# Four joined edits to a four-layer graph kernel: shared PSUM banks in the recurrent gates, and three moved steps

## The chip, the cores and the metric

One Trainium2 chip, one of its cores. The metric is device time in microseconds for one execution of the whole program. A run is timed several times and the median is given. A profile of one execution comes beside it.

## What is computed

Input x is 128 graphs of 64 nodes with 256 features, with one adjacency matrix of 64x64 for all. Four layers follow, each `x = layernorm(x + layer(x))`:

```python
x = _layernorm(x + _L0_gnn_ref(x, adj, ...))   # dense attention: softmax over neighbours
x = _layernorm(x + _L1_gnn_ref(x, ...))        # 4-head attention over 512 edges, segment softmax
x = _layernorm(x + _L2_gnn_ref(x, adj, ...))   # A_hat x, W1, batchnorm, relu, W2, batchnorm
x = _layernorm(x + _L3_gnn_ref(x, adj, ...))   # two graph convolutions, then windowed LSTMs
```

The last layer is the long one. After its two graph convolutions it runs, for each length p from 1 to 4, an LSTM over windows of p nodes and writes the last hidden state back into h:

```python
def step(carry, x_t):
    h, c = carry
    g = x_t @ Wih.T + h @ Whh.T + bias
    i, f, gg, o = jnp.split(g, 4, axis=-1)
    c = jax.nn.sigmoid(f) * c + jax.nn.sigmoid(i) * jnp.tanh(gg)
    h = jax.nn.sigmoid(o) * jnp.tanh(c)
...
for p in range(1, MAX_SKIP + 1):
    nw = Tv // p
    wins = h[:, :nw * p, :].reshape(Bv * nw, p, Hd)
    last = _lstm_last(Wih[p - 1], Whh[p - 1], bih[p - 1], bhh[p - 1], wins)
    idx = jnp.arange(nw) * p + (p - 1)
    h = h.at[:, idx, :].set(last.reshape(Bv, nw, Hd))
```

All is float32.

## The kernel before

The order of instructions is mostly written out by hand. `given` (L121 is its line) makes what it traces on an engine come after what it traced last on that engine; `step` does the same for TensorE alone in layers 0 and 1, and `behind` for one engine and its latest instruction. Where neither is used, the compiler's planner orders an engine's instructions. Each engine then works through its own list in order and waits for the others by semaphores.

**Layers 0 and 1** are one loop over 16 tiles `q` of 512 rows, with eight slots per tile. A slot has one `l1_graph` product (bank "z", two buffers) and then the steps listed in `between`. They belong to other tiles: `l0_a` to `l0_e` attention of layer 0 one or two tiles ahead, `l1_t`, `l1_qv` the projections of the next tile, `l1_softmax`, `l1_sums`, `l1_weights` once for two tiles, and `v_a`, `v_b`, `v_c` the values, the output projection with its normalisation, and layer 2's neighbour sums, a few tiles behind. Small results go through bank "m", three buffers. `v_c` fills a "z" bank and ScalarE copies it out (L491). `v_a` fills two "m" banks and ScalarE copies them out as yT (L456).

**Layer 2** is made of two products with weights, done for pairs of tiles by a Strassen-Winograd scheme: seven products in place of eight, with sums of the inputs (`tile_sums`: one subtraction on VectorE, three on GpSimd) and of the weights (`weight_sums`). While the last tiles of layer 1 end, the loop over `v_a, v_b, v_c` is filled with such products from the list `fill`. The sums use rooms that an earlier pair's sums held.

**Layer 3** begins with four blocks `gcn` of the two graph convolutions (a generator: scaling, two normalisations, neighbour sums, two products), interleaved by a hand-written list of block numbers. `first_sums` makes the weight sums of length 1 (four GpSimd subtractions, L1430) and stores them (L1432).

Then `lstm(pair)` handles 32 graphs at a time, four pairs in all. Length 1 is the class `Wide`. For lengths 2 to 4, each time step after the first has four gates f, g, i, o, a `Gate` each. A gate is again seven products: product j is made by `part(j, 0)`, with the input, and `part(j, 1)`, with the hidden state, both into one of six PSUM banks "l" (L1761). `use` then takes it out:

- products 1 and 5: ScalarE copies them to SBUF (L1776), `kept[1]` and `kept[5]`;
- product 2: VectorE adds `kept[1]` (L1778), the first quarter `t[0][:, 0]`;
- product 6: VectorE adds `kept[1]` (L1780); product 7: VectorE adds that (L1782); then `kept[5]` is added twice, for the second and fourth quarter (L1784, L1785), on GpSimd, for gate o on VectorE;
- product 4: VectorE adds `kept[7]` (L1787); product 3: VectorE adds it to the second quarter (L1789).

`act` applies sigmoid or tanh with the bias, in place (L1794), two quarters at a time; it runs in the next gate's time. `finish` and `tanh` follow with the cell. TensorE's order of the products in gates g and i is 1, 5, 2, 6, 7, 4, 3, in gate o 1, 5, 2, 6, 7, 3, 4. After gate o the first half of six products of the next step's gate f (`nxt`) is begun at once, while VectorE makes the hidden state (L1661) and its sums (L1625, L1626). Steps of other blocks (`gcn`, `final`, `prepare`) are put between gates by the table `side`.

Of the kernel before, what the change touches and what calls it, by code (L numbers as in the profile page):

```python
# [11 lines left out]
AF = mybir.ActivationFunctionType  # L12
# [7 lines left out]
N = 64  # L20
# [6 lines left out]
NQ = 16  # L27
# [14 lines left out]
def kernel(ctx: ExitStack, tc: tile.TileContext, i, out):  # L42
# [72 lines left out]
    def given(do, *args, **more):  # L115
        traced = nc.cur_bb.bb.instructions
        first = len(traced)
        with ExitStack() as order:
            for e in latest.values():
                order.enter_context(tc.issue_after(e))  # L120
            r = do(*args, **more)  # L121
        for t in traced[first:]:
            if t.engine in (mybir.EngineType.PE, mybir.EngineType.DVE, mybir.EngineType.Activation,
                            mybir.EngineType.Pool):
                latest[t.engine] = t
        return r
# [8 lines left out]
    with ExitStack() as two:  # L135
# [322 lines left out]
        def v_b(q):  # L458
# [12 lines left out]
                layernorm(x2, y, PQ, nc.gpsimd)  # L471
            nc.sync.dma_start(x2_dram[q], x2.rearrange("p c d -> p (c d)"))

        def v_c(q, one=True):

            x2 = L1.pop(q)["x2"]
            if one:
                both = bank([2, E], name="z", bufs=2)
                p_ = [both[:, s, :].rearrange("p (k c n) -> p k c n", k=KD, c=PQ) for s in range(2)]
            else:  # L480
                p_ = [bank([KD, PQ, N]) for _ in range(2)]
            for c in range(PQ):
                for k in range(KD):
                    for h in range(2):
                        for s in range(2):
                            r, f = slice(s * N, (s + 1) * N), slice(h * 64, (h + 1) * 64)
                            nc.tensor.matmul(p_[s][f, k, c, :], x2[r, c, k * P + h * 64:k * P + (h + 1) * 64],
                                             aht[r, r], start=True, stop=True)
            dst = Aq(q).rearrange("p (b s n) -> p s b n", b=KD * PQ, s=2)
            if one:  # L490
                nc.scalar.activation(dst, both.rearrange("p s (b n) -> p s b n", n=N), AF.Copy)  # L491
            else:
                for s in range(2):
                    nc.scalar.activation(dst[:, s], p_[s].rearrange("p k c n -> p (k c) n"), AF.Copy)
# [239 lines left out]
        for q in range(NQ):  # L734
            S = q // BPS - 1 if q % BPS == 0 else -1
            between = [
                [(l0_e, q + 1 if q else -1), (l0_a, q + 2)],
                [(l0_e, -1 if q else 1), (sums, q if q else -1), (l1_softmax, S)],
                [(l1_sums, S), (l0_b, q + 2)],
                [(v_b, q - LAG - 1)],  # L740
                [(l1_t, q + 1), (l1_weights, S), (l0_c, q + 2)],
                [(sums, q), (l1_qv, q + 1, 0)] + [(lambda n: behind(l0_x, n), q + 2)],
                [(v_c, q - LAG - 1), (v_a, q - LAG)],
                [(l0_d, q + 2), (l1_qv, q + 1, 1)],
            ]
            for b in range(GQ):
                step(l1_graph, q, b)
                for do, n, *more in between[b]:
                    step(do, n, *more)
                for do in setup.get((q, b), ()):  # L750
                    step(lambda _: behind(lambda _: do(), 0, mybir.EngineType.DVE), 0)
# [202 lines left out]
                    pass  # L954
            late.clear()

        def tile_sums(b):

            t2, t3, t4 = rooms[next(rooms_at) % len(rooms)]
            t1 = b(0, 1)  # L960
            given(nc.gpsimd.tensor_tensor, t3, b(1, 1), t1, OP.subtract)
            given(nc.vector.tensor_sub, t1, t1, b(0, 0))
            given(nc.gpsimd.tensor_tensor, t2, b(1, 1), t1, OP.subtract)
            given(nc.gpsimd.tensor_tensor, t4, b(1, 0), t2, OP.subtract)
            return [t1, t2, t3, t4]

        def sums_in_order(b):

# [9 lines left out]
        def inputs(q):  # L978
            return lambda k, n: Aq(q + n)[:, k * QT:(k + 1) * QT]
# [25 lines left out]
        for n, (do, q) in enumerate([(do, q) for q in range(NQ - LAG, NQ) for do in (v_a, v_b, v_c)]):  # L1005
            given(do, q, *[False] * (do == v_c))
            fill[n]()
            if n in sums_at:
                T[sums_at[n]] = tile_sums(inputs(sums_at[n]))
        q = NQ - LAST - 1  # L1010
        values.close()
        ps_b = two.enter_context(tc.tile_pool(name="ps_b", bufs=3, space=PSUM, side="right", reuse_waits="tile"))
# [28 lines left out]

        assert q == NQ - LAST - 1
        ends = range(NQ - LAST, NQ, 2)
        T = {ends[0]: tile_sums(inputs(ends[0]))}
        given(up_block, q)

        def finish(g):
# [362 lines left out]
    def gate_of(n):  # L1410
        return "ifgo".index(n), AF.Tanh if n == "g" else AF.Sigmoid
# [11 lines left out]
    def first_sums():  # L1423

        S = rooms_of(0)[1]
        a = wih1.rearrange("p k (g m c) -> p k g m c", g=3, m=2)
        a11, a12, a21, a22 = (a[:, k, :, m] for k, m in ((0, 0), (1, 0), (0, 1), (1, 1)))
        for dst, x, y, op in ((2, a11, a21, OP.subtract), (0, a21, a22, OP.add), (1, S[:, 0], a11, OP.subtract),
                              (3, a12, S[:, 1], OP.subtract)):
            nc.gpsimd.tensor_tensor(S[:, dst], x, y, op)  # L1430
        d = dram.tile([P, 3 * QT], F32, name="sums1")
        nc.sync.dma_start(d, S.rearrange("p j g c -> p (j g c)"))  # L1432
        sums_kept.append(d)

    def lstm(pair):
# [170 lines left out]
        for p in range(2, SKIP + 1):  # L1606
# [129 lines left out]
            class Gate:  # L1736


                def __init__(self, n, r, s, tiles):
                    self.n, self.r, self.s, self.tiles = n, r, s, tiles  # L1740
                    self.t = tiles[n] = rows()
                    self.banks, self.kept = {}, {}
                    self.at, _ = gate_of(n)

                def part(self, j, src):

                    if not src:
                        if j in self.banks:
                            return
                        self.banks[j] = lbank([nw, GB])  # L1750
                    r, s = self.r, self.s
                    a, S = w.raw[src], w.S[src]
                    lhs = {1: a[:, 0, self.at, 0], 2: a[:, 1, self.at, 0], 4: a[:, 1, self.at, 1]}.get(j)
                    if lhs is None:
                        lhs = S[{3: 3, 5: 0, 6: 1, 7: 2}[j]][:, self.at]
                    if j <= 3:
                        m, n = ((0, 0), (1, 0), (1, 1))[j - 1]
                        rhs = hid[:, m, n] if src else inp(r, s, m)[:, n]
                    else:
                        rhs = (hsums if src else xsums[r, s])[:, (3, 0, 1, 2)[j - 4]]  # L1760
                    nc.tensor.matmul(self.banks[j], lhs, rhs, start=src == 0, stop=src == 1)  # L1761

                def keep(self, j):
                    self.kept[j] = late.tile([P, nw, GB], F32, name="kept", bufs=5)
# [6 lines left out]

                def use(self, j):

                    b, k, t = self.banks[j], self.kept, self.t
                    if j in (1, 5):
                        nc.scalar.activation(self.keep(j), b, AF.Copy)  # L1776
                    elif j == 2:
                        nc.vector.tensor_add(t[0][:, 0], b, k[1])  # L1778
                    elif j == 6:
                        nc.vector.tensor_add(t[0][:, 1], b, k[1])  # L1780
                    elif j == 7:
                        nc.vector.tensor_add(self.keep(7), b, t[0][:, 1])  # L1782
                        e = nc.vector if self.n == "o" else nc.gpsimd
                        e.tensor_tensor(t[0][:, 1], t[0][:, 1], k[5], OP.add)  # L1784
                        e.tensor_tensor(t[1][:, 1], k[7], k[5], OP.add)  # L1785
                    elif j == 4:
                        nc.vector.tensor_add(t[1][:, 0], b, k[7])  # L1787
                    else:
                        nc.vector.tensor_add(t[0][:, 1], b, t[0][:, 1])  # L1789
# [14 lines left out]
            for r in range(len(runs)):  # L1804
                if p > 2:
                    yield "gap", unit
                for s in range(p):
# [16 lines left out]
                    else:  # L1824
                        names = "fgio"
                        for at, n in enumerate(names):
# [3 lines left out]
                            G.product(5)  # L1830
                            if prev:
                                prev.act(1)
                                prev.act(0)
                                prev.after(1)
                                G.product(2)
                                prev.after(0)
                                prev.tanh(1)
                            G.product(6)
                            if n == "o":
                                G.act(0, 0)  # L1840
                            if prev:
                                prev.tanh(0)
                            G.product(7)
# [86 lines left out]
    first = [prepare(weights_of[0, p]) for p in (2, 3)]  # L1930
    for p in (2, 3):
        weights_of[0, p].room()
    given(first_sums)
    for n in [0, 0, 0, 1, 1, 0, 1, 0, 0, 1, 2, 0, 0, 2, 1, 2, 1, 0, 3, 1, 1, 1]:
        given(next, parts[n])
    lstms = [lstm(k) for k in range(NP)]
    next(lstms[0])
    for n in [2, 3, 2, 3, 2]:
# [99 lines left out]
```

## Time and profile before

| | |
|---|---|
| median of 3 runs | 2018.45 us (2016.33 to 2020.31) |
| profiled execution | 2017.13 us |
| its span | 2015.4 us, granted TensorE clock 0.988 |
| TensorE matmul busy | 1932.2 us, 96% |
| VectorE | 1279.8 us, 64% |
| ScalarE | 952.3 us, 47% |
| GpSimd | 878.7 us, 44% |

The span goes from the first to the last instruction; the profiled execution's own time has 1.7 us more around it. Layers 0 and 1 end at about 490 us, layer 2 at about 735, and the lengths 2 to 4 of the first pair begin at about 840. In lines of the profile, "L1761 PE" is line 1761 on TensorE, PEld is TensorE's weight load, DVE is VectorE, ACT ScalarE, POOL GpSimd, SP SyncE. A tile is named out<-in, and the part in brackets is the engine's idle time before the instruction with what ended it.

### The profile page before, as it was taken

What the parts mean: (1) busy time and instruction counts of PE and PEld (TensorE: products, weight loads), DVE (VectorE), ACT (ScalarE), POOL (GpSimd) and SP (SyncE); (2) the same over time, 40 slices, a digit from 0 to 9 for tenths busy, and PEclk for the clock granted to TensorE, in tenths of its full rate; (3) what the DMA queues carried; (4) which work ended last, traced back from release to release, by engine and by line L of the source; (5) the groups of instructions that cost most, each with busy time, mean ns of one, the idle gap of its engine ahead of it and who ended that gap; (6) DMA issues with size and microseconds to landing.
All of it is one profiled execution on the core that took longest, in us unless ns stands there. A gap on an engine that the chain in (4) does not pass through costs nothing.

```text
span 2015.4 us, 31385 instructions
## 1 busy us (share of the span) xinstructions
PE 1932.2 (96%) x11447; PEld 1334.4 (66%) x11447; DVE 1279.8 (64%) x2858; ACT 952.3 (47%) x1663; POOL 878.7 (44%) x1016
## 2 busy tenths in 40 slices
PE   6899999998999989899999999999999999999996
PEld 5667777775544446577678577668577668578685
DVE  6767767664555655765657765566865557764566
ACT  4566665664336524544334644343644333544333
POOL 1133344334353633565445444345543435444264
PEclk9999999999999989999999999999999999999998
DMA  5354343322220134532333333132233032132022
GB/s 157 57 73 75 75 77 59 53 54 46 45 52 20 63 126 134 180 125 91 142 120 92 122 101 131 43 139 86 87 123 121 22 116 70 36 121 79 0 66 71
DMA packets 236538, 173.83 MB, mean 86 GB/s; under 512 B 150624, under 2 KB 213600, under 8 KB 233056
## 3 DMA queue, kind: packets, MB, share of 16 engines
q1 hardware_dynamic: 234528, 169.86, 29.9%
q8 instruction: 90, 1.47, 0.3%
q0 software_dynamic: 1024, 1.05, 0.2%
q10 hardware_dynamic: 832, 0.92, 0.1%
q14 instruction: 64, 0.52, 0.1%
HBM read 110.18 MB, written 61.60 MB: 85 GB/s over the span
## 4 chain that ended last, share of the span: by engine, by line
PE 75%; DVE 15%; ACT 3%; issue 2%; POOL 2%; DMA 2%; SPq 0%; DVEq 0%; POOLq 0%; ACTq 0%
PE l L1761 27%; PE l L1717 8%; PE pz L878 4%; PE l L1496 4%; PE m L343 3%; PE pz L807 3%; PE e L372 3%; PE z L381 2%; PE m L466 2%; PE m L346 2%; PE m L262 2%; PE g L1395 2%; PE g L1383 2%; PE pz L1076 2%; PE m L316 1%
## 5 line engine op out<-in xcount | busy, mean ns | idle before, releaser
L1761 PE MATMUL l<-hs,wh 128*128 128x256 f32 (+1 forms) x896 | 276.0, 399 | 3.7 <-DVE hs L1625 3.1
L1761 PE MATMUL l<-xs,wx 128*128 128x256 f32 (+1 forms) x896 | 276.1, 399 | 2.6 <-DVE gate L1780 2.6
L86 POOL TENSOR_TENSOR ln_rs<-ln_rs,mhalf 128x2 f32<-128x2 f32 (+2 forms) x98 | 86.3, 881 | 371.6 <-DVE ln_rs L98 365.6
L1776 ACT ACTIVATE kept<-l 128x256 f32<-128x256 f32 (+1 forms) x224 | 88.6, 402 | 333.5 <-PE l L1761 332.1
L1761 PE MATMUL l<-H,wx 128*128 128x256 f32 (+1 forms) x672 | 210.5, 402 | 4.5 <-DVE gate L1789 3.6
L1761 PE MATMUL l<-hid,wh 128*128 128x256 f32 (+1 forms) x672 | 208.8, 399 | 0.0
L1761 PEld LDWEIGHTS l<-hs,wh 128*128 128x128 f32 x896 | 169.1, 190 | 47.1 <-DVE hs L1625 5.7
L1761 PEld LDWEIGHTS l<-xs,wx 128*128 128x128 f32 x896 | 168.9, 190 | 45.7 <-POOL st L105 2.5
L1717 PE MATMUL l<-H,wx 128*128 128x256 f32 (+5 forms) x672 | 185.0, 431 | 4.9 <-DVE H L121 2.7
L1794 ACT ACTIVATE gate<-gate,bias 128x512 f32<-128x512 f32 (+1 forms) x280 | 170.6, 657 | 40.4 <-DVE gate L1785 34.5
L383 ACT ACTIVATE u<-z 128x1024 f32<-128x1024 f32 x128 | 130.2, 1024 | 75.6 <-PE z L381 74.9
L1717 PEld LDWEIGHTS l<-H,wx 128*128 128x128 f32 x672 | 118.8, 190 | 65.3 <-issue 34.4
L1761 PEld LDWEIGHTS l<-H,wx 128*128 128x128 f32 x672 | 125.7, 190 | 42.8 <-DVE gate L1789 7.6
L1761 PEld LDWEIGHTS l<-hid,wh 128*128 128x128 f32 x672 | 127.2, 190 | 32.0 <-issue 2.9
L1784 POOL TENSOR_TENSOR gate<-gate,kept 128x256 f32<-128x256 f32 (+1 forms) x84 | 65.0, 774 | 145.3 <-DVE kept L1782 144.9
L1789 DVE TENSOR_TENSOR gate<-l,gate 128x256 f32<-128x256 f32 (+1 forms) x112 | 49.9, 446 | 87.9 <-POOL gate L1784 62.1
L354 DVE TENSOR_TENSOR qs<-m,qs 64x256 fp32r<-64x256 f32 x128 | 54.0, 422 | 75.2 <-ACT qs L353 73.0
L381 PE MATMUL z<-gath_r,qs 128*128 128x512 f32 x256 | 100.6, 480 | 0.4 <-ACT u L383 0.3
L1629 POOL TENSOR_TENSOR hs<-hid 128x256 f32<-128x256 f32 (+1 forms) x28 | 26.0, 929 | 170.3 <-DVE hid L1661 87.2
L1683 ACT ACTIVATE gate<-cell 128x512 f32<-128x512 f32 (+1 forms) x88 | 58.6, 666 | 83.3 <-DVE cell L1675 60.4
L1671 POOL TENSOR_TENSOR cell<-gate,cell 128x512 f32<-128x512 f32 (+1 forms) x56 | 75.3, 1366 | 28.1 <-ACT gate L1794 28.1
L1778 DVE TENSOR_TENSOR gate<-l,kept 128x256 f32<-128x256 f32 (+1 forms) x112 | 49.1, 438 | 60.1 <-ACT gate L1794 32.7
(388 smaller groups left out, 4074.2 us busy)
## 6 DMA issues: line engine op xcount, KB each, us to landing
wx<-sums SPq DMA_DIRECT2D x9, 2048.0 KB
wh<-sums SPq DMA_DIRECT2D x9, 1792.0 KB
way<-st SPq DMA_DIRECT2D x54, 256.0 KB
st<-way SPq DMA_DIRECT2D x216, 64.0 KB
xin<-in_x SPq DMA_DIRECT2D x16, 512.0 KB
ld<-table SPq DMA_DIRECT2D x16, 512.0 KB
x_dram<-y SPq DMA_DIRECT2D x16, 512.0 KB
x2r<-x_dram SPq DMA_DIRECT2D x32, 256.0 KB
```

Of the source, the lines that this page charges most:

```text
L86: nc.gpsimd.tensor_tensor(dst, dst, mhalf[:, :n], OP.pow)
L343: nc.tensor.matmul(pq, xT[:, k, c * P:(c + 1) * P], wq[:, k, :], start=k == 0, stop=k == KD - 1)
L381: nc.tensor.matmul(z[:, k, :], L1[q]["qs"][c][:, s, k * P:(k + 1) * P], gath_r, start=True, stop=True)
L383: nc.scalar.activation(u, z, AF.Relu)
L878: nc.tensor.matmul(self.bank[at], lhs, rhs, start=first and n == 0, stop=n == len(self.terms) - 1, skip_group_check=True)
L1496: nc.tensor.matmul(self.bank[at], lhs, rhs, start=new, stop=True, skip_group_check=True)
L1671: nc.gpsimd.tensor_tensor(c, t, c, OP.mult)
L1717: nc.tensor.matmul(b, w.raw[0][:, k, at, m, :], x, start=k == 0, stop=k == KD - 1)
L1761: nc.tensor.matmul(self.banks[j], lhs, rhs, start=src == 0, stop=src == 1)
L1776: nc.scalar.activation(self.keep(j), b, AF.Copy)
L1784: e.tensor_tensor(t[0][:, 1], t[0][:, 1], k[5], OP.add)
L1794: given(lambda: nc.scalar.activation(dst, dst, f, bias=b))
```

## The change

It joins four edits.

1. Recurrent gates g, i, o (not f): product 2 is accumulated into product 1's bank after ScalarE has copied it, and product 3 into product 5's. The activation of the first quarter is taken straight from PSUM, and two additions fall away. Gate f stays as it was.
2. Layer 1: `v_c`'s copy is put behind `v_a`'s two copies on ScalarE (`v_k`), and `l0_c` changes places with `l1_weights`.
3. Layer 2: the input sums of tiles 12 and 13 are made while the last fill products run, in two parts.
4. Layer 3: the sums of `first_sums` are made after the first normalisations, and stored after the list of blocks (`keep_sums`).

```diff
+        turned_over = []
+        def v_k(q):
+            behind(lambda _: turned_over.pop(0)(), 0)
...
             if one:
-                nc.scalar.activation(dst, both.rearrange("p s (b n) -> p s b n", n=N), AF.Copy)
+                turned_over.append(lambda: nc.scalar.activation(
+                    dst, both.rearrange("p s (b n) -> p s b n", n=N), AF.Copy))
...
-                [(l1_t, q + 1), (l1_weights, S), (l0_c, q + 2)],
+                [(l1_t, q + 1), (l0_c, q + 2), (l1_weights, S)],
                 [(sums, q), (l1_qv, q + 1, 0)] + [(lambda n: behind(l0_x, n), q + 2)],
-                [(v_c, q - LAG - 1), (v_a, q - LAG)],
+                [(v_c, q - LAG - 1), (v_a, q - LAG), (v_k, q - LAG - 1)],
...
-        def tile_sums(b):
+        def sums_in_two(b):
             t2, t3, t4 = rooms[next(rooms_at) % len(rooms)]
             t1 = b(0, 1)
             given(nc.gpsimd.tensor_tensor, t3, b(1, 1), t1, OP.subtract)
             given(nc.vector.tensor_sub, t1, t1, b(0, 0))
             given(nc.gpsimd.tensor_tensor, t2, b(1, 1), t1, OP.subtract)
+            yield
             given(nc.gpsimd.tensor_tensor, t4, b(1, 0), t2, OP.subtract)
-            return [t1, t2, t3, t4]
+            yield [t1, t2, t3, t4]
...
+            if n == 6:
+                end_sums = sums_in_two(inputs(NQ - LAST))
+                next(end_sums)
+            elif n == 7:
+                T[NQ - LAST] = next(end_sums)
...
-        T = {ends[0]: tile_sums(inputs(ends[0]))}
+        T = {ends[0]: T[ends[0]]}
...
+                    self.shared = {} if n == "f" else {2: 1, 3: 5}
                 def part(self, j, src):
+                    to = self.shared.get(j, j)
                     if not src:
-                        if j in self.banks:
+                        if j in self.begun:
                             return
-                        self.banks[j] = lbank([nw, GB])
+                        self.begun.add(j)
+                        if to == j:
+                            self.banks[j] = lbank([nw, GB])
...
-                    nc.tensor.matmul(self.banks[j], lhs, rhs, start=src == 0, stop=src == 1)
+                    nc.tensor.matmul(self.banks[to], lhs, rhs, start=src == 0 and to == j, stop=src == 1,
+                                     skip_group_check=True)
...
+                    elif j == 2 and self.shared:
+                        f, by = bias_of(self.n, 0)
+                        nc.scalar.activation(t[0][:, 0], b, f, bias=by)
...
-                        e.tensor_tensor(t[0][:, 1], t[0][:, 1], k[5], OP.add)
+                        if not self.shared:
+                            e.tensor_tensor(t[0][:, 1], t[0][:, 1], k[5], OP.add)
                         e.tensor_tensor(t[1][:, 1], k[7], k[5], OP.add)
...
-                                prev.act(0)
+                                prev.act(0, 1 if prev.shared else None)
...
-                            if n == "o":
-                                G.act(0, 0)
...
-    given(first_sums)
-    for n in [0, 0, 0, 1, 1, 0, 1, 0, 0, 1, 2, 0, 0, 2, 1, 2, 1, 0, 3, 1, 1, 1]:
-        given(next, parts[n])
+    for n in [0, 0, 0, 1, 1, 0, 1, None, 0, 0, 1, 2, 0, 0, 2, 1, 2, 1, 0, 3, 1, 1, 1]:
+        given(*(first_sums,) if n is None else (next, parts[n]))
+    keep_sums()
```

More of the change, by code (lines that the diff above doesn't have):

```diff
@@ L963, in tile_sums @@
             given(nc.gpsimd.tensor_tensor, t2, b(1, 1), t1, OP.subtract)
+            yield
             given(nc.gpsimd.tensor_tensor, t4, b(1, 0), t2, OP.subtract)
-            return [t1, t2, t3, t4]
+            yield [t1, t2, t3, t4]
+        def tile_sums(b):
+            both = sums_in_two(b)
+            next(both)
+            return next(both)
         def sums_in_order(b):
@@ L1430, in first_sums, with keep_sums @@
             nc.gpsimd.tensor_tensor(S[:, dst], x, y, op)
+    def keep_sums():
+        S = rooms_of(0)[1]
         d = dram.tile([P, 3 * QT], F32, name="sums1")
@@ L1741, in __init__ @@
                     self.t = tiles[n] = rows()
-                    self.banks, self.kept = {}, {}
+                    self.banks, self.kept, self.begun = {}, {}, set()
                     self.at, _ = gate_of(n)
+                    self.shared = {} if n == "f" else {2: 1, 3: 5}
                 def part(self, j, src):
+                    to = self.shared.get(j, j)
                     if not src:
-                        if j in self.banks:
+                        if j in self.begun:
                             return
-                        self.banks[j] = lbank([nw, GB])
+                        self.begun.add(j)
+                        if to == j:
+                            self.banks[j] = lbank([nw, GB])
                     r, s = self.r, self.s
@@ L1772, in use @@
                 def use(self, j):
-                    b, k, t = self.banks[j], self.kept, self.t
+                    b, k, t = self.banks[self.shared.get(j, j)], self.kept, self.t
                     if j in (1, 5):
                         nc.scalar.activation(self.keep(j), b, AF.Copy)
+                    elif j == 2 and self.shared:
+                        f, by = bias_of(self.n, 0)
+                        nc.scalar.activation(t[0][:, 0], b, f, bias=by)
                     elif j == 2:
```

## The prediction

> **What bounds the kernel now.** I read the page's slices first, then what TensorE waits for, then the timeline around those waits, then the granted clock by stretches. Here is TensorE's row of the 40 slices (busy tenths):
>
> ```profile
> PE   6899999998999989899999999999999999999996
> ```
>
> TensorE is busy nearly everywhere. The groups show every recurrent product (four passes of 128x256, one each 0.2155 us by the starts in the timeline, so 0.86 us a product) running back to back. The change removes no matmul, so all it can win is TensorE's idle time: 2015.4 - 1932.2 = 83 us, of which about 17 lies in the first 60 us, which nothing here touches. Next, what TensorE waited for from 840 us on, the recurrent lengths (total us, times, longest):
>
> ```profile
> PE g L1918 <- DVE hd L1652: 4.1, 1, 4.1
> PE l L1761 <- DVE gate L1789: 3.6, 8, 0.6
> PE l L1761 <- DVE hs L1625: 3.1, 3, 1.2
> PE l L1761 <- DVE gate L1780: 2.6, 4, 1.0
> PE l L1717 <- DVE H L1661: 2.2, 3, 0.7
> ```
>
> With L1626 (0.6) the last four make 12.1 us, all at the end of a time step, where gate o runs out. The timeline of one such end, pair 0, length 4 (start, us, engine):
>
> ```profile
> 1078.96 0.42 DVE L1784 TENSOR_TENSOR gate<-gate,kept 128x256 f32<-128x256 f32 x1
> 1079.30 0.41 DVE L1785 TENSOR_TENSOR gate<-kept 128x256 f32<-128x256 f32 x1
> 1079.63 0.42 DVE L1789 TENSOR_TENSOR gate<-l,gate 128x256 f32<-128x256 f32 x1
> ...
> 1080.11 1.13 PE L1761 MATMUL l<-H,wx 128*128 128x256 f32 x4 [0.43 <-DVE gate L1789]
> ```
>
> VectorE works through gate o's additions without a pause, and the next step's gate f waits for banks that they hold. So gate o's tail is bound by VectorE, not by TensorE.
>
> **Recurrent gates, what goes.** Gate o loses L1778 (0.42 us) and L1784 (0.42) from VectorE, both ahead of its tail: the tail comes 0.84 us earlier (about 1.0 at length 3, where an addition takes 0.5). At pairs 0 to 2 the stalls of one end are at most 0.85, so all go: 3 x 0.19 + 3 x 0.73 + (0.43 + 0.85) + (0.64 + 0.85) + (0.43 + 0.43) = 6.4 us. At pair 3, without side work, they are 1.15, 2.15 and 2.39, and only the chain's own shift counts: 1.0 + 0.84 + 0.84 = 2.7. The final output's chain (the 4.1 us wait) gains another 0.84. Sum: 9.9 us. Gates g and i lose an addition each on VectorE (0.44) and on GpSimd (0.77); both lie beside matmuls and count for nothing themselves. ScalarE gets one half activation more per g and i (two of 0.49 for one of 0.66), at the page's 47% occupancy: nothing, as long as the copies keep their time.
>
> **Recurrent gates, what comes.** Product two now starts in product one's bank, so its first weight load waits until ScalarE's copy (L1776) has read it. Queued behind that wait on TensorE is everything. The steady case, in a gate g:
>
> ```profile
> 1087.39 0.38 ACT L1776 ACTIVATE kept<-l 128x256 f32<-128x256 f32 x1 [3.14 <-PE l L1761]
> ...
> 1087.82 0.36 PEld L1761 LDWEIGHTS l<-H,wx 128*128 128x128 f32 x2
> ```
>
> Here product two's weight load already waited on ScalarE for another reason: it started 0.05 us after the copy's end, 0.05 later than its place, and the matmul at 1087.99 lost nothing, since a load needs 0.107 us (what it takes before the next load after a stop, as at 891.50 to 891.60). So a gate pays only for what the copy's end exceeds (product two's start - 0.16 us). I lined up all 84 gates g, i, o: in 75 the copy ends 0.22 us or more before, so they pay nothing, with 0.06 us to spare. Nine, all gates i, would pay: 3 x 1.88, 2 x 0.89, 3 x 0.33, 0.26 = 8.7 us. Where the 1.88 comes from, in one of the three:
>
> ```profile
> 1375.64 0.42 DVE L1789 TENSOR_TENSOR gate<-l,gate 128x256 f32<-128x256 f32 x1 [3.40 <-POOL gate L1784]
> ...
> 1376.70 0.63 ACT L1387 ACTIVATE hT<-hT 128x512 f32<-128x512 f32 x1 [6.78 <-DVE hT L1385]
> 1377.23 0.64 ACT L1776 ACTIVATE kept<-l 128x256 f32<-128x256 f32 x2
> ```
>
> L1789 waits for GpSimd's L1784, the next block's L1385 and relu queue behind it, and the copies behind the relu. The change deletes just that L1784, so these three should fall to the 0.26 us of the same block at 864 us, where nothing held it. Charge: 3 x 0.26 + 1.78 + 0.99 + 0.26 = 3.8 us. Product three reuses product five's bank, whose copy ends 1.9 us or more earlier in every gate: nothing. Net -6.1; ends: -9.9 (no waits) and -1.2 (8.7 us of waits).
>
> The Trainium skill ("PSUM — Partial Sum Buffer", section "PSUM bank collisions raise a hardware error") says that two engines must not touch one bank and quadrant at once and that a semaphore has to guard it by bank, which speaks against this part. By that rule alone every gate could pay; the row above shows what the guard costs when the copy is punctual.
>
> **First sums of layer 3.** Four GpSimd operations (L1430, 739.47 to 743.58) stand before the first normalisation's power: its input is ready at 741.53, GpSimd takes it at 743.54, and TensorE's L1313 stands 3.47 us until 744.95. Moved behind four normalisations they run in GpSimd's gap from 753.0 to 761.9 (the first user is at 791 us), and the store L1432 goes later in SyncE's queue, past the x_dram stores and x2r loads, which loses nothing: nobody reads it before the next pair. Win: 743.54 - 741.6 = 1.9 on GpSimd, some 1.8 at TensorE.
>
> Idle there costs twice, by the granted clock (columns: stretch, its length, busy time of PE, PEld, DVE, ACT and POOL, then granted clock, DMA share, GB/s):
>
> ```profile
> 599.35:602.70 3.35, 3.35 (x5) 1.35 (x4) 2.00 (x4) 0.15 (x1) 3.35 (x4) 0.50 0.84 8
> ...
> 739.30:752.90 13.60, 9.27 (x81) 6.21 (x82) 8.83 (x31) 2.46 (x5) 10.88 (x16) 0.50 0.55 195
> ```
>
> The clock fell to half in the 3.4 us behind the 2.3 us stall at 598, and for 13.6 us here. I book 0.2 for it here (the half clock may end one 3.4 us step earlier, worth up to 1.4) and take -2.0; ends -1.0 and -3.2.
>
> The Trainium skill ("TensorE: Matmul & The Clock Gate", section "What's actually happening") has a free-running window of 3413 ns after which an idle array drops to half clock. The trace agrees, with 0.50 over stretches of 3.4 us; by that rule a stall that disappears gives back up to half a window, 1.7 us, besides itself.
>
> **Layer 2's sums.** The three GpSimd subtractions of tile 12 (1.27 each, 589.75 to 595.55) run among L898 and L904 of the last products; L904 comes at 595.51, VectorE's statistics at 596.80, L890 at 597.41, and TensorE stands 2.31 us. Moved up, two of them and the VectorE subtraction run when tile 7's last readers allow it, from 579.5 on. Win 2.3, and 0.4 to 1.7 from the half clock behind it: 1.0. Against it: the VectorE subtraction now stands before the last tile's L468 (582.77), whose normalisation reaches TensorE's L487 at 589.02 with no slack. If the subtraction waits for GpSimd's L898 or L904, that chain slips 0.7 or 1.3. I take 1.3: net -2.0; ends -4.0 and +1.0 (win of the stall lost, too).
>
> **Layer 1's loop.** The copy L491 (1.02 us on ScalarE) goes behind the two yT copies. L343 waits for a yT copy's bank six times (0.24, 0.65, 4 x 0.23 = 1.8 us); these come 1.0 us earlier and the waits go. ScalarE's total is unchanged, and the next user of L491's bank is 4 us away. With l0_c ahead of l1_weights, four additions (L276) get done before the reciprocal (1.75): exp comes earlier, which bears on one wait of 1.9 us at 126, but the transposes at L415 still wait 0.29 five times. I take 1.8 + 0.5 = -2.3; ends 0 and -4.
>
> **The sum.** -6.1 - 2.0 - 2.0 - 2.3 = -12.4 us. The profiled execution took 2017.13 (span 2015.4 and 1.7 around it); it becomes 2004.7. The median of the runs is 1.3 above the profiled one, so 2006.0.
>
> **Rivals.** *The bank's guard decides (slower).* If ScalarE puts a half activation (0.49 us) ahead of product one's copy, 0.43 us beyond the slack is paid 84 times: +36 us, 2042. It turns slower than before when copies come 0.21 us later on average (0.15 paid x 84 = 12.6). For it: the slack is only 0.06 us and ScalarE gets 56 instructions more. Against: the new activation stands after the copies and 4 us ahead of the next ones. Chance 0.11.
> *The stalls are only handed on (no change).* The tails win half (5), all 8.7 of waits stay, the three small parts bring 3.5: 2018. For: gate i's late copies are gcn blocks on ScalarE that the change leaves. Against: the deleted L1784. Chance 0.10.
> *The early sums and norms don't move up as written* (the order on GpSimd is also the compiler's planner's): layers 2 and 3 give 0, 2010. Chance 0.16.
> *Stalls and half clocks go together:* 9.0 for the gates, 3.0 for each of the two sums, 3.5 in layer 1: 2000. Chance 0.13.
>
> **How the numbers follow.** My forecast has 0.50. A measurement of this kernel tells about 0.2%, 4 us, from no change. Faster: 0.50 + 0.16 + 0.13, and 0.01 of the others, 0.80; same 0.09; slower 0.11. The range of 2000 to 2016 leaves out the slower rival, half of the no-change one and the edge of the last; the forecast's own ends are 2002 to 2010.
>
> **What would show it.** After: no TensorE waits on L1780 and L1789, L1625 about 1 us at pair 3, no wait of L1313 beyond 1.7 and none of 2.3 us in layer 2, no L343 on yT. TensorE waiting on L1776 in a handful of gates i for about 4 us is as reckoned; in tens of gates, the first rival is right, and the prediction wrong.

## The result, and the profile after

The changed kernel took 2006.56 us (median of five runs, 1999.22 to 2008.26) against 2019.36 for the kernel before, measured beside it. The ratio over all these runs (not that of the two medians, which is 0.9937) is 0.9929, with a 95% interval of 0.9916 to 0.9942. It is faster, by 0.7%; the forecast was 2006.0. The profiled execution took 2007.7 us (span 2005.9, granted clock 0.985), 9.4 less than that of before.

The engines' busy time and TensorE's 40 slices, from the page of after:

```profile
PE 1936.3 (97%) x11447; PEld 1337.8 (67%) x11447; DVE 1230.7 (61%) x2746; ACT 961.3 (48%) x1719; POOL 844.7 (42%) x960
...
PE   7899999998999989899999999999999999999997
```

TensorE's work is the same, with 4 us more of busy time, as more of it ran at half clock (below). VectorE lost 49 us and GpSimd 34, but the program gained 9: most of what they lost lay beside matmuls. What TensorE waited for from 840 us on (total us, times, longest):

```profile
PE g L1945 <- DVE hd L1672: 3.0, 1, 3.0
PE l L1785 <- DVE hs L1645: 2.3, 3, 1.0
...
PE l L1785 <- ACT kept L1801: 0.9, 2, 0.5
```

L1761 is now L1785, L1776 is L1801, L1780 L1808, L1782 L1810, L1785 L1814, L1787 L1816, L1789 L1818, L1625 L1645, L1661 L1681, L1717 L1737, L878 L884, L890 L896, L904 L910, L487 L492, L1313 L1330 and L491 L496. The waits on L1789 (3.6), L1780 (2.6), L1661 (2.2) and L1626 (0.6) are gone from this list. The end of a time step that the prediction showed at 1080.11 is now (timeline of after):

```profile
1077.24 0.42 DVE L1814 TENSOR_TENSOR gate<-kept 128x256 f32<-128x256 f32 x1
...
1077.58 0.42 DVE L1818 TENSOR_TENSOR gate<-l,gate 128x256 f32<-128x256 f32 x1
...
1078.05 0.73 PEld L1785 LDWEIGHTS l<-H,wx 128*128 128x128 f32 x4 [0.50 <-DVE gate L1818]
1078.05 1.13 PE L1785 MATMUL l<-H,wx 128*128 128x256 f32 x4
```

VectorE still works without a pause, and the weight load still waits for the addition, which ends at 1078.00. The matmul shows no idle time, but it isn't on time: it started 0.475 us after the one ahead of it and the next one 0.32 after it, where 0.2155 is the pace. So 0.36 us of the 0.70 lost here in before is still lost.

To see where the rest came from I put the starts of all 11447 matmuls of both profiles side by side, in TensorE's own order. Each number is how much a stretch of the program (by before's time) became longer or shorter, in us:

| stretch | forecast | after |
|---|---|---|
| start to 110 us (code not changed) | 0 | +3.9 |
| 110 to 504, loop of layers 0 and 1 | -2.3 | -4.2, then +1.1, then +3.6: +0.5 |
| 504 to 732, layer 2's end | -2.0 | -2.0 |
| 732 to 768, start of layer 3 | -2.0 | -1.7 |
| 854 to the end, lengths 2 to 4 | -6.1 | -10.1 |
| sum | -12.4 | -9.4 |

The first row is mostly chance: after ran 13.7 us at half clock at 22.8 us, in instructions that the change leaves alone, and before only 3.4 there. Before's profile is the shortest of all in this row: the other kernels below are 0.5 to 4.0 us longer there, three of which have nothing changed in layers 0 and 1. The stretches by granted clock (length, busy time of PE, PEld, DVE, ACT and POOL, then clock, DMA share, GB/s) show this one and those of the prediction again, in after:

```profile
22.80:36.50 13.70, 12.35 (x25) 6.91 (x26) 7.72 (x26) 4.45 (x12) 3.06 (x2) 0.50 0.00 1
...
493.90:504.10 10.20, 6.98 (x83) 3.16 (x84) 0.00 (x0) 2.92 (x4) 1.35 (x2) 0.50 0.06 23
...
599.30:602.70 3.40, 3.40 (x9) 1.52 (x8) 3.10 (x5) 1.98 (x3) 3.24 (x6) 1.00 0.65 189
739.60:753.30 13.70, 10.64 (x86) 7.52 (x87) 9.56 (x35) 3.91 (x8) 6.73 (x12) 0.50 0.52 153
```

Half clock behind layer 2's stall is gone, that of layer 3 stayed as long as it was, and there is more at the end of the loop. In all, after spent 63.4 us at half clock and before 49.3.

### The profile page after: what moved, and what is told of

It is laid out like the page before. It is cut to its first block, busy times and chain, and to the rows that moved or that the text cites. A ratio compares the mean times of both kernels' runs of the same rounds, so it can differ in the third digit from the quotient of the medians.

```text
span 2005.9 us, 31226 instructions
## 1 busy us (share of the span) xinstructions
PE 1936.3 (97%) x11447; PEld 1337.8 (67%) x11447; DVE 1230.7 (61%) x2746; ACT 961.3 (48%) x1719; POOL 844.7 (42%) x960
## 4 chain that ended last, share of the span: by engine, by line
PE 76%; DVE 12%; DMA 3%; ACT 3%; issue 3%; POOL 3%; SPq 1%; DVEq 0%; POOLq 0%; ACTq 0%
PE l L1785 31%; PE l L1737 8%; PE pz L884 4%; PE l L1516 4%; PE pz L813 2%; PE g L1412 2%; PE g L1400 2%; PE m L343 2%; PE m L346 2%; PE e L372 2%; PE pz L1093 2%; PE z L381 2%; PE m L262 2%; PE m L466 2%; PE l L1584 1%
## 5 line engine op out<-in xcount | busy, mean ns | idle before, releaser
L1785 PE MATMUL l<-hs,wh 128*128 128x256 f32 (+1 forms) x896 | 274.8, 399 | 2.3 <-DVE hs L1645 2.3
L1785 PE MATMUL l<-xs,wx 128*128 128x256 f32 (+1 forms) x896 | 275.5, 399 | 1.2 <-POOL st L105 0.9
L1801 ACT ACTIVATE kept<-l 128x256 f32<-128x256 f32 (+1 forms) x224 | 88.7, 402 | 331.5 <-PE l L1785 329.8
L1785 PE MATMUL l<-H,wx 128*128 128x256 f32 (+1 forms) x672 | 211.2, 403 | 1.6 <-ACT kept L1801 0.9
L1785 PE MATMUL l<-hid,wh 128*128 128x256 f32 (+1 forms) x672 | 208.7, 399 | 0.0
L1785 PEld LDWEIGHTS l<-hs,wh 128*128 128x128 f32 x896 | 169.6, 190 | 44.0 <-DVE hs L1645 3.6
L1785 PEld LDWEIGHTS l<-xs,wx 128*128 128x128 f32 x896 | 169.5, 190 | 43.2 <-POOL st L105 1.6
L1737 PE MATMUL l<-H,wx 128*128 128x256 f32 (+5 forms) x672 | 184.4, 431 | 2.7 <-DVE H L121 2.7
L383 ACT ACTIVATE u<-z 128x1024 f32<-128x1024 f32 x128 | 129.9, 1023 | 78.4 <-PE z L381 78.3
L1737 PEld LDWEIGHTS l<-H,wx 128*128 128x128 f32 x672 | 119.0, 190 | 62.0 <-issue 34.4
L1823 ACT ACTIVATE gate<-gate,bias 128x256 f32<-128x256 f32 (+3 forms) x252 | 143.1, 621 | 24.8 <-DVE gate L1814 20.7
L1785 PEld LDWEIGHTS l<-H,wx 128*128 128x128 f32 x672 | 124.2, 190 | 43.1 <-issue 5.7
L1785 PEld LDWEIGHTS l<-hid,wh 128*128 128x128 f32 x672 | 127.2, 190 | 32.0 <-issue 2.9
L1808 DVE TENSOR_TENSOR gate<-l,kept 128x256 f32<-128x256 f32 (+1 forms) x112 | 49.6, 442 | 144.2 <-PE l L1785 115.4
L1814 POOL TENSOR_TENSOR gate<-kept 128x256 f32<-128x256 f32 (+1 forms) x84 | 65.2, 777 | 115.3 <-DVE kept L1810 115.3
L1818 DVE TENSOR_TENSOR gate<-l,gate 128x256 f32<-128x256 f32 (+1 forms) x112 | 49.9, 446 | 54.2 <-PE l L1785 30.7
```

Source lines behind the costliest of these rows:

```text
L383: nc.scalar.activation(u, z, AF.Relu)
L1737: nc.tensor.matmul(b, w.raw[0][:, k, at, m, :], x, start=k == 0, stop=k == KD - 1)
L1785: nc.tensor.matmul(self.banks[to], lhs, rhs, start=src == 0 and to == j, stop=src == 1, skip_group_check=True)
L1823: given(lambda: nc.scalar.activation(dst, dst, f, bias=b))
```

## The experiments

The theory was the prediction's: gate o's shorter tail wins, product two's bank costs in nine gates only, and the small parts win some 2 us each. The rivals were that the bank's guard costs in every gate, and that the gain comes from another part. Stretches are given as in the table, each from one profile.

### The parts alone

**Gates alone:** before, with only the shared banks.

```diff
+                    self.shared = {} if n == "f" else {2: 1, 3: 5}
...
+                    elif j == 2 and self.shared:
+                        f, by = bias_of(self.n, 0)
+                        nc.scalar.activation(t[0][:, 0], b, f, bias=by)
...
```

> The kernel before with the shared banks of the recurrent gates alone (edit 1). Theory (the parts add up, and the gates' share is what the trace of after shows between 853 us and the end): 9.8 us less, 2009.5 against 2019.4, with TensorE waiting on the copy L1776's successor in nine to eleven gates for 3.9 us in all. Rival (the gates are worth the 6.1 us of the prediction's sum, and the rest of what came in that stretch hangs on the three moved steps): 6 us less.

Measured: 2009.53 us, ratio 0.9958 (0.9945 to 0.9972). From 854 us on it gained 9.7, nothing between 483 and 854. So the gates bring more than the 6.1 forecast.

**Layer 1's loop alone:**

```diff
+                [(l1_t, q + 1), (l0_c, q + 2), (l1_weights, S)],
...
+                [(v_c, q - LAG - 1), (v_a, q - LAG), (v_k, q - LAG - 1)],
```

> The kernel before with the two edits of layer 1's loop alone. Theory: between 110 and 450 us TensorE gains 4 us (waits for the yT copies and for the late exp go), and between 488 and 500 us it loses 0.7 us, because the last copy out of bank z now stands between the yT copies and u; how much half clock follows there is chance, so 1 to 4 us less in all. Rival (the loss at the loop's end belongs to the edit in full): no change, with 3.5 us lost between 488 and 504.

Measured: 2012.45, ratio 0.9978 (0.9969 to 0.9987). The stretch from 110 to 449 gained 8.1, that from 483 to 504 lost 3.3. The theory had 4 in the first. Of the 8.1, 1.4 is half clock that before had at 114.6 us and this profile not (the gates alone, whose loop is before's, gained 1.5 there in the same way); the other 2.7 beyond the theory stay open. At the loop's end the theory's 0.7 missed, and the loss is the rival's 3.5; the time fell all the same.

**The two early sums alone** (layers 2 and 3):

```diff
+        T = {ends[0]: T[ends[0]]}
...
+        given(*(first_sums,) if n is None else (next, parts[n]))
+    keep_sums()
```

> The kernel before with the early sums of layer 2 and the late first sums of layer 3 alone. Theory: 2.0 us less in layer 2 (4.5 won at the products, 1.7 to 2.5 lost because the last normalisation comes 1.7 us later) and 1.7 us less at the start of layer 3: 3.7 us less. Rival (the won time is half clock that falls elsewhere by chance): less than 2 us in the two stretches together.

Measured: 2014.09, ratio 0.9985 (0.9976 to 0.9994). Layer 2 -1.9, layer 3 -1.7, as in the joined kernel.

The three parts make -0.42, -0.22 and -0.15%, together -0.79%; the joined change made -0.71% (-0.84 to -0.58). The parts add up.

### Which gate wins, and which pays

**Only gate o shares its banks**, and **only gates g and i** (each is after with one line; the second has gate o's own activation call again):

```diff
-                    self.shared = {} if n == "f" else {2: 1, 3: 5}
+                    self.shared = {2: 1, 3: 5} if n == "o" else {}
```

> The kernel after, with shared banks in gate o alone; g and i as before. Theory (only VectorE's two additions ahead of gate o's tail count; the guard's waits are in gates i): the recurrent stretch stays as in after or takes 2 to 4 us less. Rival (the additions taken from VectorE and GpSimd in g and i count too): 3 to 6 us more than after.

```diff
-                    self.shared = {} if n == "f" else {2: 1, 3: 5}
+                    self.shared = {2: 1, 3: 5} if n in "gi" else {}
...
+                            if n == "o":
+                                G.act(0, 0)
```

> The kernel after, with shared banks in gates g and i alone; o as before. Theory: the tails' stalls come back and the guard's waits stay: 10 us more than after, so the recurrent stretch is as in before or longer by up to 3 us. Rival (g's and i's additions count): at most 5 us more than after.

Measured: only o, 2001.58, ratio 0.9907 (0.9886 to 0.9928); 12.5 gained from 854 on, 2.4 more than after. Only g and i, 2015.57, ratio 0.9981 (0.9971 to 0.9991), and 2.6 lost from 854 on. TensorE's waits with only o, between 853 and 1840:

```profile
PE l L1737 <- DVE H L121: 1.8, 3, 0.6
PE l L1785 <- DVE gate L1808: 0.4, 2, 0.2
PE l L1516 <- DVE hs L121: 0.4, 2, 0.2
```

and with only g and i:

```profile
PE l L1785 <- DVE gate L1818: 2.6, 6, 0.4
PE l L1737 <- DVE H L1681: 2.2, 3, 0.7
...
PE l L1785 <- ACT kept L1801: 0.9, 2, 0.5
```

The tail waits are back in the second, and the wait on product one's copy, which is in after too, is in it and not in the first. So nearly the whole gain is gate o's. In g and i the change frees VectorE and GpSimd of 56 additions each. By the starts of product two, nine gates i pay 3.5 us for it in the second kernel; as that lost 2.6 in all, the freed additions win 0.9.

### What the guard costs

**Gate i's product two behind product six** (after; two products now lie between the copy's product and product two, in place of one):

```diff
-                                G.product(2)
+                                if n != "i":
+                                    G.product(2)
...
+                            if n == "i":
+                                G.product(2)
```

> The kernel after, with product two of gate i behind product six. Theory: the bank's guard costs 3.9 us in late copies, 3.5 of it in nine gates i; with 0.86 us more for the copy these waits go and the kernel takes 3 us less than after, 9 and 13 less than before. Rival (the recurrent tail is bound by VectorE, which takes up what TensorE wins ahead of it): less than 1 us against after.

Measured: 1999.3, ratio 0.9907 (0.9892 to 0.9922). The recurrent stretch gained 13.7, 3.6 more than after, and the wait on L1801 is gone. That is 1.2 more than with gate o alone, by one profile each; by the ratios of the runs the two are alike.

**Product one copied twice** in gates g, i, o of after; the second copy writes the same values:

```diff
+                        if j == 1 and self.n != "f":
+                            nc.scalar.activation(k[1], b, AF.Copy)
```

> The kernel after, with the copy of product one made twice in gates g, i and o, so that it ends one copy later (0.26 us by the distance of two copies in a row, 0.33 at length 3). Theory (a gate pays what the copy's end exceeds product two's start less 0.16 us; the slack is 0.06 us at lengths 2 and 4): 60 gates pay 0.14 to 0.20 us and 24 pay up to 0.07, about 12 us more than after. Rival (the weight load can come later than that, and the guard has more room): no change against after.

**The same second copy in before**, where no bank is shared:

> The kernel before with the same copy made twice. There product two has a bank of its own. Theory: within 2 us of before. Rival (ScalarE's 84 additional instructions cost by themselves): some 10 us more.

Measured: after with it 2023.76, ratio 1.0019 to before (1.0009 to 1.0029): the recurrent stretch became 19.7 longer than in after. Before with it 2019.85, ratio 0.9998 (0.9986 to 1.001). The expectation for the first had the direction right, and was too small: the two copies start 0.41 us apart, so product two's bank is released that much later, not a quarter of a microsecond. The timeline of after with the second copy (L1803), one gate:

```profile
1059.97 0.38 ACT L1801 ACTIVATE kept<-l 128x256 f32<-128x256 f32 x1 [2.48 <-PE l L1785]
...
1060.38 0.38 ACT L1803 ACTIVATE kept<-l 128x256 f32<-128x256 f32 x1
...
1060.82 0.30 PEld L1785 LDWEIGHTS l<-H,wx 128*128 128x128 f32 x2 [0.49 <-ACT kept L1803]
1060.82 0.70 PE L1785 MATMUL l<-H,wx 128*128 128x256 f32 x2
```

The weight load waits, but the matmul shows no idle time. TensorE's waits of the same kernel, 855 to 1840 us, have only nine of them:

```profile
PE l L1785 <- ACT kept L1803: 4.8, 9, 0.9
```

By the distance from the last matmul's start to the next one's, every one of the 84 gates pays: 0.16 to 0.22 us at length 3, 0.29 to 0.35 at the others, up to 1.16 in gate i; 26.7 us in all, against 3.9 in after. Of these 22.8 us more, 19.7 came through to the stretch. The first rival's mechanism is real, then: a busy ScalarE makes this change slower than before, and 0.41 us was enough. In the change itself it doesn't happen.

### The loop's two edits

**The copy alone** (`v_k`) and **the exchange alone** (`l0_c` ahead of `l1_weights`), each on before:

```diff
-                [(v_c, q - LAG - 1), (v_a, q - LAG)],
+                [(v_c, q - LAG - 1), (v_a, q - LAG), (v_k, q - LAG - 1)],
```

> The kernel before with the copy out of bank z behind the yT copies alone. Theory: the waits of L343 for the yT copies go, 1.8 us and 0.27 us more for each of six (3.4 in all) less between 110 and 449 us, and 0.7 to 3 us more between 483 and 504. Rival: the wins of the loop come from the exchange of l0_c and l1_weights.

```diff
-                [(l1_t, q + 1), (l1_weights, S), (l0_c, q + 2)],
+                [(l1_t, q + 1), (l0_c, q + 2), (l1_weights, S)],
```

> The kernel before with l0_c ahead of l1_weights alone. Theory: the wait for the exp near 126 us falls from 1.9 to 0.7 (1.2 us less), L415's waits stay, and nothing changes between 483 and 504, since in the last turns there is no l0_c to exchange. Rival: most of the loop's 4 us are here.

Measured: copy 2013.54, ratio 0.9981 (0.997 to 0.9991); exchange 2018.33, ratio 1.0006 (0.9997 to 1.0016). From 110 to 449 us the copy gained 7.8, with 1.5 of half clock at 114.6 in it, where 3.4 was expected. TensorE's waits from 110 to 504 us with the copy alone no longer have L343 on yT, and have more on u:

```profile
PE m L306 <- ACT e L292: 1.9, 1, 1.9
PE e L372 <- ACT u L383: 1.9, 1, 1.9
```

with the exchange alone:

```profile
PE m L343 <- ACT yT L456: 2.3, 10, 0.2
...
PE m L306 <- ACT e L292: 0.7, 1, 0.7
```

The copy's move brings the loop's gain, and its loss at the end (+3.3 from 483 to 504, as in the joined kernel; 0.0 with the exchange). The exchange takes 1.2 us off one wait, and the time doesn't show it: L343 waits for yT ten times, 2.3 us, where before's list has five times and 1.2.

### A version made from this

After, with gate i's order as above, the copy of the loop's last turn put ahead of the yT copies again, and layer 2's VectorE subtraction put behind the last tile's normalisation:

```diff
-                [(v_c, q - LAG - 1), (v_a, q - LAG), (v_k, q - LAG - 1)],
+                [(v_c, q - LAG - 1), (v_a, q - LAG), (v_k, q - LAG - 1)] if q < NQ - 1 else
+                [(v_c, q - LAG - 1), (v_k, q - LAG - 1), (v_a, q - LAG)],
...
+            if n == 7:
+                next(end_sums)
```

> The kernel after with three places mended: product two of gate i behind product six; the last copy out of bank z (tile 11, in the last turn of the loop) back ahead of the yT copies; and of the early sums of layer 2 only the first on GpSimd stays ahead of the last normalisation, the VectorE subtraction and the second go behind it. Theory: besides the 3.6 us of the recurrent stretch that the run with gate i's order showed, 0.7 us or, with the half clock, up to 2.5 between 483 and 504, and 1.0 to 1.7 in layer 2: 1997 to 1999 where after takes 2004. Rival for the sums: the second subtraction behind the normalisation holds up the products' GpSimd additions again, and layer 2 loses 0 to 2 us instead.

Measured: 1995.83, ratio 0.989 (0.9873 to 0.9907), the fastest of all, though its interval overlaps that of gate i's order alone. From 483 to 504 it lost 1.3 in place of 3.6. TensorE's waits from 110 to 504 us:

```profile
PE m L452 <- POOL am L439: 2.4, 1, 2.4
...
PE e L372 <- ACT u L383: 1.2, 1, 1.2
```

The wait on u is back at before's 1.2, so the late copy did that; the wait on am isn't, so it did not do that. Layer 2's mend missed: -1.3 where after has -2.0. The stall at the products is back in part, 0.7 us on L896, as the rival expected. And the last normalisation comes no earlier: L492 still loses 1.7 by the starts, though the VectorE subtraction is out of its way. The GpSimd subtraction that stayed ahead holds up L910, and VectorE's statistics, which wait for that, stand before L468 (here L910 is L911 and the statistics are L999):

```profile
576.31 1.27 POOL L121 TENSOR_TENSOR lb<-A 128x512 f32<-128x512 f32 x1
577.53 1.27 POOL L911 TENSOR_TENSOR A<-wq,kept 128x512 f32<-128x512 f32 x1
...
578.84 0.69 DVE L999 BATCH_NORM_STATS2 st<-A 128x6 f32<-128x512 f32 x1 [1.76 <-POOL A L911]
579.45 1.27 DVE L468 TENSOR_TENSOR y<-m,A 128x512 f32<-128x512 f32 x2
```

## Why the prediction was right, point by point

**What bounds the kernel** held: gate o's tail on VectorE. Sharing in gate o alone gains 12.5 us, and in g and i alone it loses 2.6.

**What goes in the gates** had the right places and was too small. Net -10.1 against -6.1, and 3.9 of waits as charged, so the gross gain was 14.0 and not 9.9. Pair 3 and the end of the program made 4.1 against 3.5; pairs 0 to 2 made 10.0 against 6.4. The term that was mis-sized is the sum of recorded idle times. At 1080.11 before shows 0.43 of idle, but that matmul started 0.81 us after the one ahead of it, and the next one 0.32, where 0.2155 is the pace: 0.70 lost. A matmul is recorded 0.38 long, 0.16 beyond its place in the row, which hides as much of any wait; and behind the stop the next matmul comes some 0.10 late, as its weight load isn't hidden. So a wait in such a row costs 0.27 more than its recorded idle time.

By the starts, the gain at pairs 0 to 2 is 1.8 at the three waits on L1626 (0.6 in the prediction's sum), 2.5 at the three on L1661 (2.2), 4.2 at the eight on L1780 and L1789 (3.6), and 1.2 at a wait of 0.82 on L1731 at 891.5, which the sum left out. "So all go" was wrong for the eight: they cost 5.7 in before, but five of them still cost 0.35 to 0.38 each in after, as at 1078.05 above. One sign missed too: L1625 was to fall to about 1 us at pair 3, and its successor L1645 shows 2.3. Two of its three waits stayed at 0.97, and the shift came out at the stops ahead of them.

The Trainium skill ("TensorE: Matmul & The Clock Gate", section "Single matmul latency") gives a single bf16 matmul at full clock a constant of 166 ns beyond its columns, mostly for the array to drain. The trace has the same 0.16 in its float32 rows, but the profile models the ends of matmuls, so this is no second measurement; the starts are.

**What comes in the gates** was right in size and place: 3.94 us against 3.8, with 0.00 in 73 gates. The nine gates i paid 3 x 0.26, 0.26, 3 x 0.33 and 2 x 0.74, and two others 0.21 each. The three of 1.88 fell to 0.26, as they should with L1784 gone. Product three paid nothing in any of the 84, as forecast. This sum was made from starts, not from idle times, and so was right where the other was short. One of them, in after:

```profile
1172.96 0.64 ACT L1801 ACTIVATE kept<-l 128x256 f32<-128x256 f32 x2
...
1173.38 0.30 PEld L1785 LDWEIGHTS l<-H,wx 128*128 128x128 f32 x2 [0.87 <-ACT kept L1801]
1173.38 0.70 PE L1785 MATMUL l<-H,wx 128*128 128x256 f32 x2 [0.47 <-ACT kept L1801]
```

Recorded 0.47, lost 0.74. In the list of waits this place and its like make 0.9 in all.

**Layer 3** was -1.7 against -2.0. The wait of 3.47 became 1.6, as forecast; the half clock that I booked 0.2 for stayed at 13.7 us.

**Layer 2** was -2.0 as forecast, from parts that were each larger than booked. The subtraction waited for GpSimd, took 1.74 us where it took 0.69 in before, and stands before L468:

```profile
586.55 1.74 DVE L121 TENSOR_TENSOR A<-A 128x512 f32<-128x512 f32 x1 [0.53 <-POOL lb L121]
...
594.28 2.06 PE L492 MATMUL m<-aht,y 64*64 64x64 f32 x64 [0.80 <-POOL y L105]
```

L492 lost 1.65 (1.3 charged); the stall brought 2.6 (2.3), the full clock behind it 1.7 (1.0); and smaller waits took 0.6 back. The 1.7 is in part luck: layer 1's loop alone has the same stall of 2.3 us, and its profile shows no half clock behind it, while four other kernels with that stall have the 3.4 us at 0.50 that before has.

The Trainium skill ("TensorE: Matmul & The Clock Gate", section "What's actually happening") has half clock after an idle window of some 3.4 us. The trace agrees on the length, with 0.50 for 3.4 us at 599.3 in before, and not on the idle time: the stall ahead of it was 2.3 us. At 739.6 two microseconds less idle changed nothing.

**The loop** failed: +0.5 in the profile, against -2.3. The gain from 110 to 449 was there, 4.2, and larger than booked: by the starts the six waits of L343 gave 2.8 (1.8) and the earlier exp 1.2 (0.5). The step that failed is that the copy's move costs nothing at the end. There its bank isn't the question, its place is. In before L491 ran at 492.14, while ScalarE had nothing else to do. In after (timeline):

```profile
493.31 1.89 POOL L439 COPY am<-ld 128x1024 f32<-128x1024 f32 x1 [1.00 <-DMA ld<-table]
495.25 1.98 PE L452 MATMUL m<-am,v 64*64 64x64 f32 x64 [2.42 <-POOL am L439]
...
498.26 1.03 ACT L496 ACTIVATE A<-z 128x1024 f32<-128x1024 f32 x1
...
500.26 1.08 PE L372 MATMUL e<-u,apad 128*32 128x512 f32 x4 [1.87 <-ACT u L383]
```

L496 waits in line behind the yT copies, ahead of L383, whose u TensorE needs: 0.7 us. L439 came 1.0 later against TensorE, since its load landed later, and 1.84 were half clock. In all seven profiles of kernels with the late copy this stretch lost 2.9 to 4.5, with 10.2 us at half clock. Of the four other kernels with the copy always in its old place, three had 3.4 us there, as before has, and lost at most 0.2; the fourth, before with the second copy of product one, had 10.2 too and lost 2.5. So the loss goes with the copy, but half clock at that place also comes by itself. The late load isn't needed for it: the loop alone and the kernel with only g and i lost 3.3 and 2.9 with the wait on am at before's 1.4. Only the 0.7 is settled as the copy's own; why the half clock is longer stays open.

So that the median came out 0.6 from the forecast is in part luck. In the profile the change is worth 9.4 and not 12.4: 4 us more from the gates, about 3 lost against the forecast in the loop, and 4 of chance in the first 110 us, where before's profile is the shortest. The medians, 12.8 apart, don't rest on that one profile.

## What to carry to other kernels

Count a wait of a pipelined engine from start to start, never by the idle time in the list: here 84 waits, most of some 0.3 us, showed as nine. Where an addition is taken away, ask which engine ends the step's chain: gate o's two additions on VectorE were worth 12.5 us, and those taken out of gates g and i won 0.9 and brought 3.5 of waits. A bank shared in time costs only what its reader exceeds the other work between the two uses, so put that work there.

## What the runs showed of the hardware

The same instructions ran with half clock at different places from one execution to the next: 3.4 to 13.7 us of it near 25 us, in code that no kernel here touched, and 46 to 63 us in all in the profiled executions of the kernels above. Those 17 us at half clock are worth some 8, as much as the edits of layers 1 to 3 together (0.37% of 2017 is 7.5), so one profile can't price these. The second is the size of what a stop hides: 0.27 us for each wait in a row of 128x256 products, 0.16 that the recorded length of the matmul ahead covers and 0.10 behind the stop.
